# Layer 0 of a graph network: softmax weights and two operands of the counts held in a PSUM bank

## The chip, the cores and the metric

The kernel runs on one core of one Trainium2 chip, in one launch. The metric is device time in microseconds, the median of the timed runs. The engines are TensorE (PE in the profile, its weight loads PEld), VectorE (DVE), ScalarE (ACT), GpSimd (POOL) and SyncE (SP), which here only starts DMAs. Gathers by index are started by POOL.

## The reference, cut to what matters

Four graph layers run one after the other over 3125 nodes with 128 features and 100000 edges sorted by their destination. Each layer's result is added to its input and normalised. The change touches the first layer alone, a softmax-weighted sum over the edges that enter a node and the node itself:

```python
pre_edge = hP1[dst] + hP2[src] + zP3[edge_type]
logit_edge = _leaky(pre_edge) @ y_w                       # 8 heads
logits = jnp.concatenate([logit_self, logit_edge], axis=0)
mx = jax.ops.segment_max(logits, dst_a, num_segments=n)
ex = jnp.exp(logits - mx[dst_a])
denom = jax.ops.segment_sum(ex, dst_a, num_segments=n)
alpha = ex / denom[dst_a]
t_edge = hWh[src] + zWz[edge_type]
msg = (alpha[:, :, None] * t).reshape(-1, D)              # t in 8 heads of 16
agg = jax.ops.segment_sum(msg, dst_a, num_segments=n)
out = _leaky(agg + residual_weight * h)
```

The second layer averages node rows over the edges. The kernel computes it with a dense matrix of edge counts, which it builds while the first layer runs ("the counts").

## The kernel before, in words

The nodes are sorted by degree into 25 tiles of 128, one node a partition. Tile `t` has room for `CAP[t]` edges a node, 57 in the first and 21 in the last, 821 in all. A tile's edges are cut into chunks of at most 8 (`W`), 114 in all, and the chunks into runs of two or three, 49 in all.

For each edge of a chunk POOL starts one gather of 128 node rows into the tile `hs` (lines 102, 1207 and about). Each row holds 128 values for the attention, 128 values to be weighted and 8 logit parts. The relation rows `z` come in one of two ways: 77 chunks ("mult") make them by TensorE from one-hot matrices, the others gather them as `zs`, 205 gathers in all. TensorE adds up `pre`, ScalarE applies the leaky part, TensorE makes the 8 logits of each edge in PSUM (`lg`). VectorE adds the rest of a chunk's logits into the run's SBUF buffer `lgs` (L1360).

For a whole run `flow_run` then adds the mask (L1370), appends the node's old maximum as one more column (L1373), takes the new maximum (L1375), subtracts it (L1378) and lets ScalarE take the exponential in place (L1380). So `lgs` then holds `n` columns of 8 weights and, as column `n`, the factor `corr` for what was summed before. VectorE reads these: each chunk's values are multiplied by their weights (L970, in `spread`) and halved into one sum (L959, L963), which is added to the tile's sum (L1403); the tile's older sum is faded by `corr` (L833), the weights are summed into `sm` (L1391) and the denominator `l` is brought up to date (L1392, L1394).

Beside it `counts` builds the count matrix tile by tile. In `part_a` VectorE compares source numbers with all blocks (L615), runs a scan over the flags that counts them (L620), makes a base for each block from a matmul (L636, L639), adds it to the counts (L641), masks (L643) and reduces (L646). In `one_hots` (L568) VectorE compares digits with an index row `up` that lies in a PSUM tile, written by two TensorE transposes at the start (`count_up`) and from then on read by VectorE alone.

The order of the work on VectorE, ScalarE and TensorE in this layer is written out by hand. Each flow is a generator; `Plan.run` takes the one that is due first, lets it issue instructions until its next `yield`, and puts it back that many units later. `Room(n)` counts buffers: a flow that takes one while none is free is put back until another gives one. This decides the order of instructions when the kernel is built; on the chip each engine runs its queue in that order and waits for data. POOL and SP are not under this order.

```python
            A.activation(lgm, lgm, AF.Exp)
            yield 4
            corr = run.lg[:, n, :]
            for i, k in enumerate(run.chunks):
                plan.soon(1.5 * i, flow_spread(k))
```

Of the kernel before, what the change touches and what calls it, by code (L numbers as in the profile page):

```python
# [9 lines left out]
F32 = mybir.dt.float32  # L10
F16 = mybir.dt.float16
BF16 = mybir.dt.bfloat16
I32 = mybir.dt.int32
AF = mybir.ActivationFunctionType
OP = mybir.AluOpType
AX = mybir.AxisListType
# [3 lines left out]
P = 128  # L20
N = 3125
NT = 25
# [6 lines left out]
W = 8  # L29
# [5 lines left out]
H = 8  # L35
# [8 lines left out]
OFF = [sum(CAP[:t]) for t in range(NT + 1)]  # L44
NS = OFF[NT]
# [42 lines left out]
def tile_gnn(ctx, tc, a, out):  # L88
    nc = tc.nc
    V, A, G, T = nc.vector, nc.scalar, nc.gpsimd, nc.tensor  # L90
# [407 lines left out]
    with tc.tile_pool(name="srcp", bufs=1) as sp, tc.tile_pool(name="srcq", bufs=2, space=PSUM) as ps:  # L498
# [8 lines left out]
        for t in range(NT):  # L507
# [6 lines left out]
                                   op0=OP.add, op1=OP.mult)  # L514
            V.scalar_tensor_tensor(srcs[:, sl], pay_sb[:, sl, 0], float(-NP), live[:, :CAP[t]],
                                   op0=OP.add, op1=OP.mult)
# [10 lines left out]
        for o in range(0, NS, P):  # L527
            n = min(P, NS - o)
# [13 lines left out]
    blk0 = {}  # L542
# [8 lines left out]
    def count_up(pool, of):  # L551

        ri = pool.tile([P, 1], I32, name="c_ri")
        V.tensor_copy(ri, rowid)
        V.tensor_scalar(ri, ri, 1, None, op0=OP.arith_shift_right)
        rf = pool.tile([P, 1], F32, name="c_rf")
        V.tensor_copy(rf, ri)
        for k in range(2):
            row = pool.tile([P, P], BF16, name="c_row", bufs=2)
            V.tensor_scalar(row, onesb, rf, float(k * P // 2), op0=OP.mult, op1=OP.add)  # L560
            T.transpose(of[:, k * P:(k + 1) * P], row, identb)
        return of.rearrange("p (d s) -> p d s", s=2)
# [41 lines left out]
                if wait is not None:  # L604
                    self.soon(wait, steps)

    def counts(plan, begins, cp, ps, up, misc):


        def part_a(t):  # L610
            n, nb = CAP[t], NB[t]
            sl = slice(OFF[t], OFF[t + 1])
            oh = cp.tile([P, NT * max(CAP)], BF16, name="c_oh")[:, :NT * n]
            oh3 = oh.rearrange("p (j s) -> p j s", s=n)
            V.tensor_tensor(oh3, srchi[:, sl].unsqueeze(1).to_broadcast([P, NT, n]),  # L615
                            each_j[:, :, :n], op=OP.is_equal)
            yield 3
            inc = cp.tile([P, NT * max(CAP)], F32, name="c_inc")[:, :NT * n]
            inc3 = inc.rearrange("p (j s) -> p j s", s=n)
            V.tensor_tensor_scan(inc, oh, oh, 0.0, op0=OP.add, op1=OP.max)  # L620
            yield 4
            end = cp.tile([P, NT + 1], F32, name="c_end")
            G.memset(end[:, 0:1], 0.0)
            V.tensor_copy(end[:, 1:], inc3[:, :, n - 1])
            yield 3
            cnt = cp.tile([P, NT], BF16, name="c_cnt")
            V.tensor_sub(cnt, end[:, 1:], end[:, :NT])
            yield 3
            yield from misc.take()
            pre = ps.tile([P, 2, NT], F32, name="c_pre", tag="misc")  # L630
            T.matmul(pre[:, 0, :], upperb, cnt, start=True, stop=True)
            T.matmul(pre[:, 1, :], onesb, cnt, start=True, stop=True)
            yield 3
            V.scalar_tensor_tensor(crowd, pre[:, 1, :], float(-nb * P), crowd, op0=OP.add, op1=OP.max)
            bs = cp.tile([P, NT], F32, name="c_bs")
            V.tensor_sub(bs, pre[:, 0, :], end[:, :NT])  # L636
            misc.give()
            yield 3
            V.tensor_add(bs, bs, blk0[nb])  # L639
            yield 3  # L640
            V.tensor_add(inc3, inc3, bs.unsqueeze(2).to_broadcast([P, NT, n]))  # L641
            yield 3
            V.tensor_mul(inc3, inc3, oh3)  # L643
            yield 3
            pos = cp.tile([P, max(CAP)], F32, name="c_pos")
            V.tensor_reduce(pos[:, :n], inc.rearrange("p (j s) -> p s j", s=n), AX.X, OP.add)  # L646
            yield 4
            posi = cp.tile([P, max(CAP)], I32, name="c_posi")
            V.tensor_scalar(posi[:, :n], pos[:, :n], -1.0, None, op0=OP.add)
            yield 3  # L650
            dig = cp.tile([P, 2, max(CAP)], I32, name="c_dig")
            V.tensor_scalar(dig[:, 0, :n], posi[:, :n], 127, None, op0=OP.bitwise_and)
            V.tensor_scalar(dig[:, 1, :n], posi[:, :n], 7, None, op0=OP.arith_shift_right)
            yield 3
            digb = cp.tile([P, 2, max(CAP) + max(CAP) % 2], BF16, name="c_digb", bufs=2)
            V.tensor_copy(digb[:, :, :n], dig[:, :, :n])
            return digb
# [229 lines left out]
    with tc.tile_pool(name="l0", bufs=2) as wp, tc.tile_pool(name="l0s", bufs=1) as sp, \  # L887
# [78 lines left out]
        def spread(ac, hs, ex, n):  # L966

            val = hs[:, :n, D:2 * D]
            valh = val.rearrange("p s (h d) -> p s h d", h=H)
            V.tensor_tensor(valh, valh, ex.unsqueeze(3).to_broadcast([P, n, H, D // H]), op=OP.mult)  # L970
            yield 2.5
            yield from halves(hs[:, :, D:2 * D], n)
# [22 lines left out]
                except StopIteration as e:  # L995
                    return e.value

        up = count_up(cp, ps1.tile([P, 2 * P], BF16, name="c_up"))
        lg_at = ps1.tile([P, 2, 3 * W, H], F32, name="lg")
        misc = Room(1)  # L1000

# [148 lines left out]
        plan = Plan()  # L1150
        owns, selves, hws, hqs, azs, zbs, xs, shuts, x1s = map(Room, (1, 2, 3, 3, 4, 3, 5, 2, 3))
        hss, zss_, rbs, ohs_, zTs, zhs, zpss, pres, lows, tps, lgss = map(Room, (8, 3, 2, NK + 2, 2, 1, 1, 2, 2, 1, 3))
# [6 lines left out]
        class Run:  # L1159
            def __init__(self, tile_, k, run, behind_):  # L1160
                self.tile, self.k, self.behind, self.chunks = tile_, k, behind_, []
                self.s0, self.s1 = run[0][0], sum(run[-1][:2])
                self.n, self.lg, self.ex = self.s1 - self.s0, None, None
                self.summed = self.topped = self.totalled = False
                self.adds, self.faded = 0, False

        class Chunk:
            def __init__(self, run, s0, w, mult, g, start):
# [9 lines left out]
        for t in range(NT):  # L1178
            c = Tile(t)
# [3 lines left out]
            for run in runs(t):  # L1183
# [3 lines left out]
                for s0, w, mult in run:  # L1187
                    k = Chunk(R_, s0, w, mult, g, now)
# [5 lines left out]
        whole = now  # L1194
# [171 lines left out]
        def flow_run(run):  # L1366
            c, n, t = run.tile, run.n, run.tile.t
            o = OFF[t] + run.s0
            lg, lgm = run.lg[:, :n], run.lg[:, :n + 1]
            V.tensor_add(lg, lg, mask[:, o:o + n].unsqueeze(2).to_broadcast([P, n, H]))  # L1370
            while run.behind is not None and not run.behind.topped:
                yield 0.5
            V.tensor_copy(run.lg[:, n, :], m[:, t, :])  # L1373
            yield 2.5
            V.tensor_reduce(m[:, t, :], lgm.rearrange("p s h -> p h s"), AX.X, OP.max)  # L1375
            run.topped = True
            yield 2.5
            V.tensor_sub(lgm, lgm, m[:, t, :].unsqueeze(1).to_broadcast([P, n + 1, H]))  # L1378
            yield 1.5
            A.activation(lgm, lgm, AF.Exp)  # L1380
            yield 4
            corr = run.lg[:, n, :]
            for i, k in enumerate(run.chunks):
                plan.soon(1.5 * i, flow_spread(k))
            yield 1
            while run.behind is not None and (run.behind.adds or not run.behind.totalled):
                yield 0.5
            faded(c.ac, corr, H)
            run.faded = True
            sm = wp.tile([P, H], F32, name="sm")  # L1390
            V.tensor_reduce(sm, run.lg[:, :n].rearrange("p s h -> p h s"), AX.X, OP.add)  # L1391
            V.tensor_mul(l[:, t, :], l[:, t, :], corr)  # L1392
            yield 2.5
            V.tensor_add(l[:, t, :], l[:, t, :], sm)  # L1394
            run.totalled = True

        def flow_spread(k):
            run = k.run
            c, at = run.tile, k.s0 - run.s0
            yield from spread(c.ac, k.hs, run.lg[:, at:at + k.w], k.w)  # L1400
            while not run.faded:
                yield 0.5
            V.tensor_add(c.ac, c.ac, k.hs[:, 0, D:2 * D])  # L1403
            hss.give()
            run.adds -= 1
            if not run.adds:
                while not run.totalled:
                    yield 0.5
                lgss.give()
                if run is c.runs[-1]:  # L1410
                    while not c.self_done:
                        yield 1
                    plan.soon(2.5, close_b(c))
# [4 lines left out]
        for k in chunk_list:  # L1418
# [8 lines left out]
            for i in range(len(k.parts())):  # L1427
                plan.go(k.start + 1 + 4.5 * i, flow_pre(k, i))
            plan.go(k.start + 18, flow_lg(k))
        counts(plan, [0.95 * whole * OFF[t] / NS - 70 for t in range(NT)], cp, ps1, up, misc)  # L1430
        with tc.manual_schedule(engines=ORDERED | {mybir.EngineType.PE}):
            plan.run()
        assert hss.free == 8 and lgss.free == 3 and misc.free == 1 and shuts.free == 2 and x1s.free == 3
# [8 lines left out]
    with ExitStack() as ctx1, tc.tile_pool(name="l1", bufs=2) as wp, tc.tile_pool(name="l1s", bufs=1) as sp:  # L1442
# [14 lines left out]
        with tc.If(general > 0):  # L1457

            with tc.tile_pool(name="l1g", bufs=1) as gp, tc.tile_pool(name="l1gp", bufs=1, space=PSUM) as ps:
# [13 lines left out]
                for t in range(NT):  # L1473
# [6 lines left out]
                    with tc.For_i(0, trips, 1):  # L1480
# [10 lines left out]
                        at = gp.tile([P, W], F32, name="at")  # L1491
# [22 lines left out]
        ps1 = ctx1.enter_context(tc.tile_pool(name="l1p", bufs=1, space=PSUM))  # L1514
# [20 lines left out]
        with tc.tile_pool(name="l1pay", bufs=1) as pp:  # L1535
# [3 lines left out]
            for h in range(H2):  # L1539
                for k in range(3):  # L1540
                    V.scalar_tensor_tensor(bias[:, :, h], pays.bitcast(F32)[:, :, 3 + k],
                                           we[:, k * H2 + h:k * H2 + h + 1], mask if k == 0 else bias[:, :, h],
                                           op0=OP.mult, op1=OP.add)
# [574 lines left out]
```

## Time and profile before

| what | us |
|---|---|
| median of 3 timed runs | 5276.86 |
| lowest and highest of them | 5252.7 and 5283.75 |
| the profiled execution | 5264.1 |
| its span, first to last instruction | 5262.1 |
| busy in the span: PE, PEld | 2142.5, 1406.3 |
| busy in the span: DVE, ACT, POOL | 2924.2, 983.1, 2851.4 |

One execution was profiled. The page gives each engine's busy time, the span cut into 40 slices, and the costliest groups of instructions with their number, their mean duration and the idle time before them. A group is named by line, engine, operation and tiles, as out<-in; buffer numbers are left out. L102 is the helper that starts every gather, so gathers are told apart by their tiles. "remote" or "issue" as the cause of idle time means that the profile shows no instruction that ended the wait. Some matmul records are missing, so TensorE does somewhat more than its rows show.

### The profile page before, as it was taken

To read this page: it belongs to the slowest core of one execution; us is meant where nothing else is said; L and a number is where in the kernel's file an instruction comes from. 1 tells how busy PE (TensorE), PEld (TensorE's weight loads), DVE (VectorE), ACT (ScalarE), POOL (GpSimd) and SP (SyncE) were. 2 spreads that over 40 slices of the span, in tenths; PEclk is the share of its full clock that TensorE was granted. 3 is DMA by queue.
4 is the path that set the end of the run, shared out by engine and by line. 5 is a ranking of instruction groups with operands and counts; after the bars stand their busy time and mean duration, and the time that the engine had idled before them with its cause. 6 is when DMAs were issued, how large, how long until landed. Compare 5 with 4: busy or idle time off the path is not lost. (4 is left out here: it accounts for less than half of the span.)

```text
span 5262.1 us, 40042 instructions
## 1 busy us (share of the span) xinstructions
PE 2142.5 (41%) x12091; PEld 1406.3 (27%) x12091; DVE 2924.2 (56%) x6838; ACT 983.1 (19%) x2505; POOL 2851.4 (54%) x2922
## 2 busy tenths in 40 slices
PE   7166667677756677666480022222334000000000
PEld 5154545445544445444240011111111000000000
DVE  8355656566655566565523456656665355554555
ACT  1122233233323233322110011111111000000000
POOL 0544545546454344444217756666662777777774
PEclk9577788778777778777695555555557555555555
DMA  3422333333232222323343333333332333333331
GB/s 83 123 75 79 86 85 92 90 84 108 79 94 75 73 83 83 82 79 94 135 148 106 101 95 105 114 107 114 116 112 82 105 98 93 92 93 92 92 93 49
DMA packets 215514, 498.36 MB, mean 95 GB/s; under 512 B 62393, under 2 KB 112364, under 8 KB 210649
## 3 DMA queue, kind: packets, MB, share of 16 engines
q0 software_dynamic: 136448, 397.65, 26.7%
q1 hardware_dynamic: 78808, 97.76, 5.9%
q8 instruction: 102, 1.67, 0.1%
q14 instruction: 156, 1.28, 0.1%
HBM read 424.65 MB, written 70.63 MB: 94 GB/s over the span
## 5 line engine op out<-in xcount | busy, mean ns | idle before, releaser
L102 POOL DMA_INDIRECT hs<-h_tab,srcx x821 | 826.2, 1006 | 634.0 <-issue 395.7
L102 POOL DMA_INDIRECT kv<-ktv_tab,idx x821 | 852.5, 1038 | 283.5 <-issue 265.1
L102 POOL DMA_INDIRECT kv<-kv_tab,srcx x821 | 781.6, 952 | 368.3 <-issue 252.4
L1594 DVE TENSOR_TENSOR kv<-kv,qp 128x1024 f32<-128x1024 f32 (+4 forms) x228 | 253.1, 1110 | 694.7 <-DMA kv<-ktv_tab,idx 453.8
L102 POOL DMA_INDIRECT zs<-z_tab,rel x205 | 221.8, 1082 | 389.2 <-DVE zs L986 91.5
L1605 DVE TENSOR_REDUCE u<-kv 128x128 f32<-128x1024 f32 (+4 forms) x228 | 383.7, 1683 | 26.1 <-issue 19.7
L1248 PE MATMUL zps<-oh,zq 128*128 128x512 bf16 x1232 | 362.7, 440 | 57.0 <-issue 38.6
L568 DVE TENSOR_TENSOR c_ohs<-c_ends,c_up 128x1024 bf16<-128x1024 bf16 (+3 forms) x196 | 115.7, 591 | 315.8 <-remote 200.6
L949 PEld LDWEIGHTS pre<-ident,hs 128*128 128x128 f32 x1642 | 254.2, 219 | 130.0 <-issue 120.5
L1318 PE MATMUL t_ps<-zw,zT 128*128 128x136 f32 x1232 | 225.1, 318 | 155.8 <-DVE hs L1327 115.6
L949 PE MATMUL pre<-ident,hs 128*128 128x128 f32 x1642 | 256.6, 302 | 27.0 <-issue 24.3
L1597 DVE TENSOR_REDUCE lg<-kv 128x32 f32<-128x1024 f32 (+5 forms) x228 | 251.7, 1104 | 22.4 <-issue 22.2
L1601 DVE TENSOR_TENSOR kv<-kv,ex 128x1024 f32<-128x1024 f32 (+4 forms) x228 | 251.3, 1102 | 11.7 <-issue 11.7
L953 PE MATMUL lg<-yw,low 128*128 128x8 f32 x1642 | 238.8, 269 | 40.1 <-issue 24.2
L953 PEld LDWEIGHTS lg<-yw,low 128*128 128x128 f32 x1642 | 241.9, 222 | 48.6 <-issue 26.2
L678 ACT ACTIVATE c_oha<-c_oha,srclo 128x50 bf16<-128x50 bf16 (+2 forms) x821 | 211.7, 347 | 208.3 <-DVE c_oha L568 145.5
L1327 DVE TENSOR_TENSOR hs<-hs,t_ps 128x408 f32<-128x408 f32 (+1 forms) x231 | 121.2, 525 | 213.6 <-remote 58.4
L1318 PEld LDWEIGHTS t_ps<-zw,zT 128*128 128x128 f32 x1232 | 184.4, 214 | 183.1 <-issue 79.8
L837 PE MATMUL tp<-ident,an 128*128 128x128 f32 x25 | 11.3, 454 | 534.3 <-remote 465.1
L943 PE MATMUL pre<-identb,hq 128*128 128x512 bf16 (+3 forms) x645 | 205.8, 433 | 12.1 <-issue 12.1
L751 ACT ACTIVATE c_sb<-c_ps 128x512 bf16<-128x512 f32 (+1 forms) x175 | 96.3, 550 | 582.5 <-remote 259.1
L747 PE MATMUL c_ps<-c_ohs,c_ohd 128*128 128x128 bf16 x1300 | 127.0, 243 | 172.3 <-ACT c_sb L751 83.0
(418 smaller groups left out, 4785.2 us busy)
## 6 DMA issues: line engine op xcount, KB each, us to landing
rb<-rel_tab SPq DMA_DIRECT2D x77, 256.0 KB
c_tab<-c_sb SPq DMA_DIRECT2D x25, 768.0 KB
cs<-c_tab SPq DMA_DIRECT2D x6, 3200.0 KB
hs<-h_tab,srcx POOLq DMA_INDIRECT x821
kv<-kv_tab,srcx POOLq DMA_INDIRECT x821
kv<-ktv_tab,idx POOLq DMA_INDIRECT x821
h_tab<-h SPq DMA_DIRECT2D x25, 132.0 KB
zs<-z_tab,rel POOLq DMA_INDIRECT x205
```

What stands on the lines that cost most here:

```text
L102: return G.indirect_dma_start(out=dst, out_offset=None, in_=table, in_offset=indirect(idx), **kw)
L678: A.activation(oha[:, s // 2, 0, :, s % 2], oha[:, s // 2, 1, :, s % 2], AF.Copy, scale=srclo[:, o:o + 1])
L747: T.matmul(cps[:, j * P:(j + 1) * P], ohd[:, b // 2, :, b % 2], ohs[:, b // 2, :, b % 2], start=(i == 0), stop=(i == nb - 1))
L943: T.matmul(pre[:, :k], hq[:, i, :], identb.unsqueeze(1).to_broadcast([P, k, P]), start=(i == 0), stop=False)
L949: T.matmul(pre[:, s, :], hs[:, s0 + s, :D], ident, start=False, stop=(s == k - 1))
L953: T.matmul(lg_ps[:, s, :], low[:, s, :], yw8, start=True, stop=True)
L1248: T.matmul(zps, zq[:, i, 2 * R * k2:2 * R * (k2 + 1)], k.hot[i][:, cols], start=(i + k2 == 0), stop=(i == NK - 1 and k2 == 1))
L1318: T.matmul(t_ps[:, s, :], k.zT[:, (s0 + s) * P:(s0 + s + 1) * P], zw[:, D:], start=True, stop=True)
L1594: V.tensor_mul(k, k, qp.unsqueeze(1).to_broadcast([P, n, D]))
L1597: V.tensor_reduce(lg, kv[:, :n, :D].rearrange("p s (h d) -> p s h d", h=heads), AX.X, OP.add)
L1601: V.tensor_tensor(v, v, ex.unsqueeze(3).to_broadcast([P, n, heads, D // heads]), op=OP.mult)
L1605: V.tensor_reduce(u, kv[:, :n, D:].rearrange("p s d -> p d s"), AX.X, OP.add)
```

## The change

The index row's PSUM tile becomes a whole bank of 512 four-byte elements a partition. Its first 128 hold the index row as before. Three other things that VectorE reads come to lie in it:

- the weights of one run, `ex_at`. After the exponential, VectorE copies all `n + 1` columns of `lgs` there (up to 200 elements a partition). The multiplications, the fade, the sum and the product read the copy. Since there is room for one run, `exs = Room(1)` is taken before the copy and given back when the run's multiplications are issued and `l` is up to date. The `lgs` buffer is given back right after the copy, no longer after the run's last addition;
- the base `bs_at` of the counts, 25 elements, which one addition writes and the next reads;
- the scan's second operand. It was the flags themselves; it is now the first element of the index row, 0, repeated. The scan's second operation is a maximum, so the count, never below 0, is the same with either.

```diff
-            V.tensor_tensor_scan(inc, oh, oh, 0.0, op0=OP.add, op1=OP.max)
+            V.tensor_tensor_scan(inc, oh, up[:, 0, 0:1].to_broadcast([P, NT * n]), 0.0, op0=OP.add, op1=OP.max)
...
-            V.tensor_add(bs, bs, blk0[nb])
+            V.tensor_add(bs_at, bs, blk0[nb])
             yield 3
-            V.tensor_add(inc3, inc3, bs.unsqueeze(2).to_broadcast([P, NT, n]))
+            V.tensor_add(inc3, inc3, bs_at.unsqueeze(2).to_broadcast([P, NT, n]))
...
-        up = count_up(cp, ps1.tile([P, 2 * P], BF16, name="c_up"))
+        own_bank = ps1.tile([P, 4 * P], F32, name="c_up")
+        up = count_up(cp, own_bank.bitcast(BF16)[:, :2 * P])
+        ex_at = own_bank[:, P:P + (3 * W + 1) * H].rearrange("p (s h) -> p s h", h=H)
+        bs_at = own_bank[:, 3 * P:3 * P + NT]
+        exs = Room(1)
...
             A.activation(lgm, lgm, AF.Exp)
             yield 4
-            corr = run.lg[:, n, :]
+            yield from exs.take()
+            V.tensor_copy(ex_at[:, :n + 1], lgm)
+            lgss.give()
+            corr = ex_at[:, n, :]
...
-            V.tensor_reduce(sm, run.lg[:, :n].rearrange("p s h -> p h s"), AX.X, OP.add)
+            V.tensor_reduce(sm, ex_at[:, :n].rearrange("p s h -> p h s"), AX.X, OP.add)
...
             run.totalled = True
+            weights_read(run)
+
+        def weights_read(run):
+            if run.totalled and not run.mults:
+                exs.give()
...
-            yield from spread(c.ac, k.hs, run.lg[:, at:at + k.w], k.w)
+            steps = spread(c.ac, k.hs, ex_at[:, at:at + k.w], k.w)
+            yield next(steps)
+            run.mults -= 1
+            weights_read(run)
+            yield from steps
...
-                lgss.give()
```

More of the change, by code (lines that the diff above doesn't have):

```diff
@@ L605, in run, with counts @@
                     self.soon(wait, steps)
-    def counts(plan, begins, cp, ps, up, misc):
+    def counts(plan, begins, cp, ps, up, bs_at, misc):
         def part_a(t):
@@ L1164, in __init__ @@
                 self.summed = self.topped = self.totalled = False
-                self.adds, self.faded = 0, False
+                self.adds, self.mults, self.faded = 0, len(run), False
         class Chunk:
@@ L1429, in tile_gnn @@
             plan.go(k.start + 18, flow_lg(k))
-        counts(plan, [0.95 * whole * OFF[t] / NS - 70 for t in range(NT)], cp, ps1, up, misc)
+        counts(plan, [0.95 * whole * OFF[t] / NS - 70 for t in range(NT)], cp, ps1, up, bs_at, misc)
         with tc.manual_schedule(engines=ORDERED | {mybir.EngineType.PE}):
```

## The prediction, made before the changed kernel was run

> **What bounds the kernel now.** I read the busy time by stage first, since the change touches Layer 0 alone. The stages were cut at the first gather of node rows and at the last write of the layer's rows. Columns: length, then busy microseconds and instruction count of each engine, granted TensorE clock, DMA share, GB/s.
>
> ```profile
> core 0: us, PE busy (x) PEld busy (x) DVE busy (x) ACT busy (x) POOL busy (x), PEclk, DMA share, GB/s
> 0.00:200.00 200.00, 107.06 (x1002) 86.10 (x1002) 148.52 (x462) 20.91 (x70) 34.06 (x81) 0.85 0.34 99
> 200.00:2551.00 2351.00, 1569.28 (x9845) 1111.69 (x9845) 1358.94 (x3880) 693.65 (x1861) 1082.10 (x1100) 0.77 0.31 84
> ...
> 2900.00:3950.00 1050.00, 263.77 (x453) 115.20 (x453) 624.93 (x1188) 129.15 (x262) 699.16 (x733) 0.55 0.36 108
> 3950.00:5262.10 1312.10, 53.20 (x125) 23.92 (x125) 666.81 (x1008) 112.69 (x220) 885.08 (x853) 0.52 0.31 89
> ```
>
> Layer 0 is the 2351 us row. TensorE is busy 67% of it, VectorE 58%, POOL 46%. The last two rows are Layers 2 and 3, where POOL leads with 67%. So POOL, the engine this change can relieve, is third in the stage where it is to be relieved. The chain that ended last says nothing here: it lies in Layer 3.
>
> Second, what TensorE waited for inside that stage (who, by whom, total, times, longest):
>
> ```profile
> PE t_ps L1318 <- DVE hs L1327: 115.6, 54, 12.3
> PE c_ps L747 <- ACT c_sb L751: 83.0, 21, 15.9
> ...
> PE sl_ps L1068 <- DVE rest L1139: 28.8, 2, 22.2
> ...
> PE pre L949 <- DMA hs<-h_tab,srcx: 1.7, 1, 1.7
> ```
>
> TensorE idles 2351 - 1569 = 782 us. Adding up all lines of this view that name VectorE gives about 260 us, a third. Gathered rows ended 1.7 us of it, and 5.3 us before the weight loads of the same line. Counted over the 734 first uses of gathered rows between 260 and 2310 us, the rows had landed a median of 12 us before TensorE took them. Late gathers are not what Layer 0 waits for.
>
> Third, the gathers by duration (min/median/max in ns), and one place in the order of time where they are slowed:
>
> ```profile
> L102 POOL DMA_INDIRECT hs<-h_tab,srcx x821: 940/946/2825, 199.3 to 2456.2; - x165
> L102 POOL DMA_INDIRECT kv<-kv_tab,srcx x821: 940/946/1543, 2767.5 to 3941.6; - x165
> ```
>
> ```profile
> 1004.38 1.21 DVE L970 TENSOR_TENSOR hs<-hs,lgs 128x1024 f32<-128x1024 f32 x1
> ...
> 1005.14 1.61 POOL L102 DMA_INDIRECT hs<-h_tab,srcx  x1 [0.30 <-issue]
> 1005.52 0.41 DVE L959 TENSOR_TENSOR zh<-zh 128x256 f32<-128x256 f32 x1
> ...
> 1007.05 0.95 POOL L102 DMA_INDIRECT hs<-h_tab,srcx  x1 [0.30 <-issue]
> ```
>
> A gather needs 0.946 us. The one that ran beside two VectorE instructions with both inputs in SBUF took 1.61 us; the next, alone, 0.95. The page has the mean of the 821 `hs` gathers at 1006 ns and of the 205 `zs` gathers at 1082. The 821 of Layer 2, where the weights already come from PSUM, have 952. So the effect the change aims at exists. VectorE itself is not held up: its group `hs<-hs,lgs` shows no idle time before it.
>
> **The change, part by part.** Fourth, VectorE groups with their shapes (busy us, mean ns, then idle before):
>
> ```profile
> L970 DVE TENSOR_TENSOR hs<-hs,lgs 128x1024 f32<-128x1024 f32 x92 | 111.9, 1216 | 0.0
> L1601 DVE TENSOR_TENSOR kv<-kv,ex 128x1024 f32<-128x1024 f32 x184 | 222.4, 1209 | 6.6 <-issue 6.6
> L1360 DVE TENSOR_TENSOR lgs<-lg,hs 128x64 f32<-128x64 f32 x92 | 19.8, 215 | 19.1 <-remote 13.3 <-PE c_perm L688 3.2 <-PE lg L953 1.5
> L989 DVE TENSOR_TENSOR az<-az,zs 128x64 f32<-128x64 f32 x37 | 7.9, 214 | 0.0
> L1378 DVE TENSOR_TENSOR lgs<-lgs,m 128x200 f32<-128x200 f32 x14 | 5.0, 359 | 0.0
> L1864 DVE COPY xqb<-qkv 128x128 f32<-128x128 f32 x25 | 6.1, 243 | 13.6 <-ACT qkv L1852 13.4
> ```
>
> *Added: one copy a run.* There are 49 runs (L1373 stands 49 times). The copy has the shape of the subtraction on L1378, whose 49 took a median of 292 ns: 49 x 0.292 = 14.3 us is the upper end. No copy into PSUM is in the trace. The lower end is L1373's 8-element copy, 169 ns: 8.3 us. Between 169 ns at 8 elements and 243 at 128 the mean copy of 142 elements costs 0.25 us; I take 0.27, nearer to the row of its own shape, so 13 us. A neighbour that reads what was just written starts 0.03 us after its end in the records, an unrelated one 0.08 us before it: 0.11 x 49 = 5.7 us at most, and 3 taken, as other work often stands between. Together 16 us of VectorE, between 8 and 20. Everything behind the copy in VectorE's fixed order waits too, above all the `hs` addition L1327 that gives TensorE its `t_ps` buffer back. The wait for the exponential only moves from the first multiplication to the copy in front of it.
>
> *Moved to PSUM: 114 multiplications, 49 fades, 49 sums, 49 products.* L970 against L1601 is the same shape with the small operand in SBUF and in PSUM: 1216 and 1209 ns. At 64 elements L989 and L1360 say 214 and 215. So 0, between -1 and +1 us. [...]
>
> *The counts' base:* 25 additions of 25 elements that write PSUM, 25 additions (25.2 us) that read it. 0 by the same pairs of rows.
>
> *The scan:* 25 instructions, 46.5 us, 1247 to 3128 ns from 525 to 1425 elements, so 2.09 ns an element, where the additions on L641 take 1.06 (1062 to 1646 ns from 875 to 1425). If the second stream is what doubles it, a one-element operand saves up to 21 us; if PSUM is dear there, a few us are added. The scan at L286, with other types, has the same slope (425 ns for 128), so I take 0 and keep -21 to +3.
>
> *The gathers.* All that could be lost to VectorE in the stage is (1006 - 946) x 821 + (1082 - 946) x 205 = 77 us. Laying each gather over the VectorE rows it overlapped, the excess falls to L970 (about 15 us), the scan (14) and L641 (7): 36 us that POOL would save. The halving additions, the `zs` additions and others keep both inputs in SBUF and the rest of the excess. [...] On TensorE's path lie 1.7 + 5.3 us of waits for landings; I take 3 us of gain, between 0 and 36.
>
> *The room for one run's weights and the earlier return of the logits' buffer.* Neither alters the written order: in the trace each run's last multiplication and its update of `l` end before the next run's first multiplication starts, and by the written due times a logits buffer is free whenever a run takes one. 0. If the room bound, the next run's copy, and in the written order all that follows it, would stand behind the earlier run's update of `l`, 3.4 us after its first multiplication in the first run.
>
> **Sum.** VectorE's 16 us reach the end in part: a third by its share of TensorE's idle time, all of it where the chain runs through VectorE. I take half, +8, between +3 and +20. Less 3 for gathers: +5 us. The profiled execution took 5264.1 us (span 5262.1 and 2.0 around it), 12.8 below the median of the three timed runs, 5276.86, which themselves spread over 31 us. 5264.1 + 5 = 5269, or 5282 from the median; I forecast the middle, 5276.
>
> **Rivals.**
> *Faster:* POOL's saving counts in full and the scan loses its second stream: 36 + 21 - 8 = 49 us, 5227. For it: the lengthened gathers at 1004 us, and Layer 2's 952 ns. Against it: 12 us of slack and 7 us of waits for landings. It needs more than 53 us to leave the 1% band, so also gathers that now queue behind one another; 0.12.
> *Slower:* POOL's order. DVE, ACT and PE are in hand-written order, POOL and SP are not; 49 new copies may shift where a POOL instruction that waits for VectorE stands among the gathers. The clearing of `x` (L909) already waits 84.3 us for VectorE in 7 places, 27.0 at the longest, with gathers queued behind. With 12 us of slack one more such wait costs TensorE up to 15 us; from four on it passes 53 us: 5276 + 60 = 5336. Nothing in the diff touches those instructions, so 0.14.
> *The change doesn't do what it says:* `hs` gathers stay at 1006 ns, as other both-in-SBUF work takes the place. Then +8 instead of +5, 5279; this is inside the forecast's band, 0.15 of its 0.74.
>
> **How the numbers follow.** 1% (53 us) is about what a measurement of this kernel can tell from no change. Forecast and third rival 0.74, faster 0.12, slower 0.14. The range runs from 5276 - 40 (the gathers' 36 us on the path and copies nearly hidden) to 5276 + 34 (all 20 us of copies on the path, and one displaced POOL wait of 14): 5236 to 5310.
>
> **What would show it.** Right: 49 copies of 0.25 to 0.30 us into `c_up`; L970's successor within 20 ns of 1216; the `hs` mean near 970 ns; POOL some 36 us less busy in Layer 0; that stage within 25 us of 2351; Layers 1 to 3 alike. Wrong: a stage shorter by over 50 us with TensorE's waits for VectorE much smaller, which would mean that the gathers held the stage in a way the waits don't show; or longer POOL waits at L909 and TensorE waiting for landings.

## The result, and the profile after

The change took 5308.12 us, the median of six runs (5307.16 to 5326.16), against 5269.37 us for the kernel before in the same comparison. The ratio is 1.0088 with a 95% interval of 1.0065 to 1.0112: slower by 39 us between the medians, and by 46 us (34 to 59) by the ratio and its interval, where +5 was worked out. The time lies in the predicted range and the ratio within 1%, but the rise is real and the sum does not explain it. The profiled execution of the changed kernel is the longest of the six, 5326.16 us with a span of 5324.2; the one of before took 5264.1. So the two profiles lie 62 us apart, further than the medians.

The busy time by stage, with the same columns as before the change:

```profile
core 0: us, PE busy (x) PEld busy (x) DVE busy (x) ACT busy (x) POOL busy (x), PEclk, DMA share, GB/s
0.00:200.00 200.00, 107.18 (x1002) 86.09 (x1002) 148.57 (x460) 21.13 (x70) 34.31 (x81) 0.85 0.34 99
200.00:2614.00 2414.00, 1587.55 (x9845) 1128.78 (x9845) 1368.43 (x3925) 693.97 (x1861) 1051.64 (x1099) 0.76 0.30 82
...
4010.00:5324.20 1314.20, 51.84 (x125) 23.17 (x125) 667.66 (x1008) 112.70 (x220) 888.03 (x854) 0.52 0.31 89
```

Layer 0 is 2414 us, 63 more than in the profile before; the last two layers are as they were. In it VectorE is 9.5 us busier, POOL 30.5 us less busy. Of VectorE's time the 49 copies are 14.8 us. The 49 sums of the weights, which now read the copy, give 4.7 us back (18.9 before, 14.2 after). Both edits show up, and neither is near 63 us.

The gathers (min/median/max in ns), two VectorE groups with their shapes (busy us, mean ns, then idle before), and the sums before and after (min/median/max in ns):

```profile
L102 POOL DMA_INDIRECT hs<-h_tab,srcx x821: 943/949/2132, 199.1 to 2529.6; - x165
...
L102 POOL DMA_INDIRECT zs<-z_tab,rel x205: 943/949/1850, 201.7 to 2516.5; - x103
```

```profile
L970 DVE TENSOR_TENSOR hs<-hs,c_up 128x1024 f32<-128x1024 f32 x92 | 111.8, 1215 | 0.6
...
L833 DVE TENSOR_TENSOR az<-az,c_up 128x128 f32<-128x128 f32 x49 | 13.7, 280 | 0.0
```

```profile
L1391 DVE TENSOR_REDUCE sm<-lgs x49: 270/376/500, 332.4 to 2527.5; 128x8 f32<-128x192 f32 x14, 128x8 f32<-128x128 f32 x13, 128x8 f32<-128x72 f32 x4, 128x8 f32<-128x120 f32 x3
...
L1398 DVE TENSOR_REDUCE sm<-c_up x49: 226/284/357, 331.9 to 2592.8; 128x8 f32<-128x192 f32 x14, 128x8 f32<-128x128 f32 x13, 128x8 f32<-128x72 f32 x4, 128x8 f32<-128x120 f32 x3
```

The longest `hs` gather fell from 2825 to 2132 ns, the mean of the 821 from 1006 to 990 and that of the 205 `zs` gathers from 1082 to 1007. The multiplications take 1215 ns as against 1216. The 49 copies (L1387) take 0.30 us each.

What grew stands in the list of waits (who, by whom, total us, times, longest), first two lines of before and then those of the change:

```profile
ACT c_sb L751 <- remote: 259.1, 29, 19.3
...
DVE c_ohs L568 <- remote: 200.6, 23, 18.0
```

```profile
ACT c_sb L751 <- remote: 377.8, 36, 20.6
DVE c_ohs L568 <- remote: 255.0, 23, 17.5
...
PE c_ps L747 <- ACT c_sb L751: 105.4, 22, 16.0
...
PE t_ps L1322 <- DVE hs L1331: 92.4, 44, 15.1
```

The last two were 83.0 and 115.6 before: TensorE's wait for VectorE, through which the copies were expected to act, fell. The two largest waits for which the profile names nobody grew by 119 and 54 us. Two others of the kind fell, ScalarE's `low` (L1300, now L1304) from 154.0 to 126.0 and VectorE's `c_ohb` (L568) from 150.3 to 114.1, so the list alone does not say what the layer lost. In order of time, one of those that grew:

```profile
2330.04 0.91 PE L1322 MATMUL t_ps<-zw,zT 128*128 128x136 f32 x6
...
2331.13 0.95 POOL L102 DMA_INDIRECT hs<-h_tab,srcx  x1 [0.30 <-issue]
2332.39 0.94 POOL L102 DMA_INDIRECT hs<-h_tab,srcx  x1 [0.31 <-issue]
...
2341.14 0.95 POOL L102 DMA_INDIRECT hs<-h_tab,srcx  x1 [0.30 <-issue]
2342.09 0.22 POOL L909 MEMSET x<- 128x128 f32 x1
2342.24 0.12 POOL L623 MEMSET c_end<- 128x1 f32 x1
2342.59 1.01 POOL L102 DMA_INDIRECT x<-in_x,node_d  x1 [0.23 <-POOL c_end L623]
2346.32 0.60 ACT L751 ACTIVATE c_sb<-c_ps 128x512 bf16<-128x512 f32 x1 [19.08 <-remote]
2346.32 0.69 DVE L568 TENSOR_TENSOR c_ohs<-c_ends,c_up 128x1024 bf16<-128x1024 bf16 x1 [17.29 <-remote]
...
2346.97 0.80 PE L747 MATMUL c_ps<-c_ohs,c_ohd 128*128 128x128 bf16 x6 [16.02 <-ACT c_sb L751]
```

From 2331 to 2346 us nothing runs on TensorE, VectorE or ScalarE, while POOL starts one gather after another until 2343.6 us. ScalarE's copy L751 waits for matmuls that had ended by 2331 us; it starts 2.7 us after POOL's last gather has ended. I call this a standstill: time in Layer 0 (from the first `hs` gather to the last write of the layer's rows) in which none of PE, PEld, DVE and ACT has a record. Added up over the layer, from the records:

| kernel | Layer 0 | standstill | the rest |
|---|---|---|---|
| before | 2347 | 433 | 1914 |
| the change | 2412 | 492 | 1920 |

The part in which some engine works is 6 us longer, as the prediction's sum has it. The other 59 us are standstill. The prediction's reading had no such item: it counted idle time engine by engine, and none of its sums uses a wait for "remote".

### The profile page after: what moved, and what is told of

Same layout as the page of the kernel before. It is cut to its first block, busy times and chain, and to the rows that moved or that the text cites. A ratio compares the mean times of both kernels' runs of the same rounds, so it can differ in the third digit from the quotient of the medians.

```text
span 5324.2 us, 40114 instructions
## 1 busy us (share of the span) xinstructions
PE 2155.9 (40%) x12091; PEld 1420.4 (27%) x12091; DVE 2931.2 (55%) x6887; ACT 983.7 (18%) x2505; POOL 2825.3 (53%) x2922
## 5 line engine op out<-in xcount | busy, mean ns | idle before, releaser
L102 POOL DMA_INDIRECT hs<-h_tab,srcx x821 | 812.6, 990 | 676.2 <-issue 439.9
L102 POOL DMA_INDIRECT zs<-z_tab,rel x205 | 206.5, 1007 | 421.8 <-DVE zs L986 101.2
L949 PEld LDWEIGHTS pre<-ident,hs 128*128 128x128 f32 x1642 | 260.7, 223 | 150.4 <-issue 138.8
L568 DVE TENSOR_TENSOR c_ohs<-c_ends,c_up 128x1024 bf16<-128x1024 bf16 (+3 forms) x196 | 115.9, 593 | 329.5 <-remote 255.0
L949 PE MATMUL pre<-ident,hs 128*128 128x128 f32 x1642 | 265.3, 307 | 40.2 <-issue 38.9
L751 ACT ACTIVATE c_sb<-c_ps 128x512 bf16<-128x512 f32 (+1 forms) x175 | 96.3, 551 | 697.8 <-remote 377.8
```

What stands on the lines that cost most here:

```text
L102: return G.indirect_dma_start(out=dst, out_offset=None, in_=table, in_offset=indirect(idx), **kw)
L949: T.matmul(pre[:, s, :], hs[:, s0 + s, :D], ident, start=False, stop=(s == k - 1))
```

## The experiments

The runs fell into two kinds of job. In the first kind the kernel before takes 5269 to 5312 us, in the second 4333 to 4339, with the same program. VectorE and ScalarE are equally busy in both (1359 and 694 us of Layer 0 in the first profile, 1357 and 690 in `e5`); TensorE (1569 and 1390 us) and the `hs` gathers (1006 and 1116 ns) are not. The expectations speak of two kinds of chip; since a job of either kind named chip number 8, the runs do not tell whether the kind belongs to the chip, its machine or the hour. A ratio is always against before in the same job.

### Which part costs it (first kind, before 5298.62 us)

`e1`: the weights' copy and its readers, with scan and base as before:

```diff
-            V.tensor_add(bs_at, bs, blk0[nb])
+            V.tensor_add(bs, bs, blk0[nb])
...
-            V.tensor_tensor_scan(inc, oh, up[:, 0, 0:1].to_broadcast([P, NT * n]), 0.0, op0=OP.add, op1=OP.max)
+            V.tensor_tensor_scan(inc, oh, oh, 0.0, op0=OP.add, op1=OP.max)
```

> The weights' copy and their readers as in the change; scan and counts' base as before. This kernel has the 49 copies, and its SyncE order is that of before (the whole change has one pair swapped there: the last piece of a count row stands behind the load of a later tile's sums). Theory C, the copies cost the whole rise because every wait between VectorE, TensorE and ScalarE behind them is stretched: +35 to +45 us against before, Layer 0 as long as with the change. Theory S, the swapped pair on SyncE costs most of it: +5 to +15 us here. Theory P, reading the weights from PSUM is dear: as C here, but not where the copies go unread.

5327.48 us, ratio 1.0057 (1.0040 to 1.0074): +29 us.

`e2`: the kernel before with only the copy added (`V.tensor_copy(ex_at[:, :n + 1], lgm)` behind the exponential).

> The kernel before with the 49 copies into the PSUM bank added; nothing reads them, all readers use lgs, and the lgs buffer is given back as before. SyncE order as before. Theory C: +30 to +45 us, as much as the copies with their readers. Theory P (PSUM readers are dear): +5 to +15 us. By the prediction's term for the copies: +3 to +20 us. Theory S: +5 to +15 us. The hs gathers stay near 1006 ns here, since the multiplications keep both inputs in SBUF.

5309.26 us, 1.0020 (1.0004 to 1.0036): +11 us. `hs` gathers at 1009 ns, as before.

`e3`: scan and base from PSUM, no copies; `e4`: the scan's operand alone, the diff's scan line and nothing else.

> Scan operand and counts' base from the PSUM bank, weights as before: no copy. It has the swapped pair on SyncE. Theory S: +25 to +40 us. Theory C: 0 to +5 us. By the prediction's terms for both: -21 to +3 us, taken as 0.

> Only the scan's second operand is the one PSUM element; order of every engine, SyncE too, as before. All theories 0 within 5 us; if the scan's operand matters, its 25 instructions (46.5 us) change by up to 20 us and the time with them, and the gathers beside the scan come to 0.95 us each.

`e3` 5340.31 us, 1.0076 (1.0047 to 1.0105); `e4` 5333.85 us, 1.0066 (1.0047 to 1.0084): +35 us. This answered none of the theories. In `e4` no instruction is added, the order on every engine is that of before, and the 25 scans take 46.4 us in all as against 46.5. Beside longer standstills, the difference that its records show is in the gathers beside the scan: `hs` 989 ns on average. The base and the swapped pair on SyncE, which `e3` has and `e4` has not, make 6 us between the medians, less than the intervals can tell. Theories C, P and S fell. Nor do the parts add up: `e1` and `e3` together make 71 us, the whole change made 39 in its job.

### Is it the change at all? (second kind, before 4332.97 us)

`e5` is the kernel before against itself. `e6` is `e4` with the element in an SBUF tile of zeros (`none[:, 0:1]` for `up[:, 0, 0:1]`), `e7` the base alone, `e8` the whole change.

> The kernel before, unchanged, as a control, with a profile from the same chip as the experiments. The four kernels run so far, even the one that only changed the scan's operand, lag behind the first profile of before in the same staircase (about +10 us by 515 us, +30 by 985 us). Theory K (the changes cause the lag): ratio 1.000, and this profile runs as the first one, within 5 us at 985 us. Theory N (the lag belongs to the execution, not to the change): this profile shows part of the staircase too, 10 to 30 us at 985 us. Theory L (each load of a program has its own time, and differences of 0.5% mean nothing): the ratio leaves 1.000 by over 0.003.

> As the run that changed the scan's operand alone, but the one element lies in SBUF (a tile of zeros) instead of PSUM. Same order on every engine. If the PSUM operand cost the +35 us: within 5 us of before. If what costs is that the scan no longer streams two SBUF operands and the gathers beside it get quicker: +30 to +40 us, hs gathers near 990 ns. If it was no effect of the operand at all: anything.

> Only the counts' base goes to the PSUM bank; scan and weights as before. It has the swapped pair on SyncE. If the pair is what cost in the run with scan and base: +35 to +45 us. If the scan is: 0 to +10 us.

> The whole change once more on the chip of the experiments. The first comparison gave 1.0088 (1.0065 to 1.0112). If the parts add, scan +35, base and swap +6, copies and weights +30: +70 us, 1.013. If they share one cause that can cost only once: +35 to +50 us.

0.9992 (0.9983 to 1.0000), 0.9993 (0.9982 to 1.0004), 0.9979 (0.9970 to 0.9987) and 0.9987 (0.9978 to 0.9995). In this kind of job the change costs nothing that the control doesn't show as well. Layer 0 of `e5`, and under it that of `e8`:

```profile
199.00:1872.00 1673.00, 1389.67 (x9842) 1024.11 (x9842) 1357.13 (x3873) 689.67 (x1859) 1193.55 (x1099) 0.89 0.43 118
```

```profile
199.00:1862.00 1663.00, 1412.80 (x9843) 1039.56 (x9843) 1364.25 (x3919) 690.02 (x1860) 1091.82 (x1098) 0.88 0.44 119
```

VectorE is as busy as in the first profile (1357 and 1359 us), yet the layer is 674 us shorter. The standstill is 51 us here and 35 with the change, against 433 in the first profile, which makes 382 of the 674 us. In the rest TensorE is busy for 1390 us instead of 1569 with the same instructions, at a granted clock of 0.89 instead of 0.77. The list of waits of `e5` names a releaser nearly everywhere: ScalarE's `c_sb` waits 320.0 us for `c_ps` and none for "remote". The relief of the gathers is far larger than in the first profile: more of them overlap VectorE in the shorter layer (125 of the 1026 overlap nothing of it, 497 in the first profile), POOL drops by 102 us (`hs` 1116 to 1025 ns, `zs` 1173 to 1046), and still the time gains nothing that could be told from the control, with TensorE 83 and 85% busy and VectorE 81 and 82%. The swapped pair on SyncE, which `e7` has, costs nothing here (0.9979). With the one SBUF element (`e6`) `hs` stays at 1114 ns as against 1116, so that operand brings no relief.

### The controls once more (first kind, before 5298.05 us)

`e9` is before against itself, `e10`, `e11` and `e12` are `e4`, `e2` and `e1` again.

> The kernel before against itself once more. Two kinds of chip have shown up: one on which before takes 5270 to 5300 us, and one on which it takes 4333 us; the control has run only on the second (0.9992). If this job falls on the first kind: theory K (the parts cause the +0.6 to +0.9% seen there) wants 1.000 within 0.002; theory L (every load of a program has its own time there) wants a ratio off 1 by over 0.003 either way. On the second kind: 1.000 within 0.001.

> Scan's second operand alone from PSUM, a second time. On the first kind of chip: 1.0066 again by theory K, anything between 0.997 and 1.008 by theory L. On the second kind: same order, same durations of its scans, gathers beside them shorter; 0 to -10 us, and hs gathers some 30 us of POOL shorter in all (there the mean was 1116 ns before and 1025 with the whole change).

> The 49 copies into the PSUM bank that nobody reads. On the first kind: 1.002 again by theory K. On the second kind VectorE is busy for over 80% of Layer 0, so most of the copies' 13 to 18 us should show: +8 to +18 us (1.002 to 1.004); by the prediction's term +3 to +20; 0 if TensorE alone sets the time there. Gathers as before (near 1116 ns).

> Copies and their readers, scan and base as before. On the first kind: 1.0057 again by theory K. On the second kind: as the unread copies, less what the quicker gathers give back: the difference between the two is the whole worth of the relief. By the prediction -3 us (0 to -36); hs gathers near 1050 ns.

1.0005 (0.9986 to 1.0024), 1.0033 (1.0013 to 1.0053), 1.0021 (1.0002 to 1.0040) and 1.0038 (1.0021 to 1.0056). The control lies on 1, the parts do not. But the scan alone came out at 15 us where it had been 35, so between two jobs of this kind a ratio moves by 0.3%, more than its interval says. Layer 0 taken apart for all profiles of this kind:

| kernel | Layer 0 | standstill | the rest | `hs`, `zs` mean ns |
|---|---|---|---|---|
| before, `e9` before | 2347, 2384 | 433, 464 | 1914, 1920 | 1006, 1082; 1013, 1100 |
| copies unread: `e2`, `e11` | 2388, 2392 | 462, 451 | 1926, 1941 | 1009, 1070; 1015, 1077 |
| weights: `e1`, `e12` | 2413, 2393 | 495, 478 | 1918, 1915 | 999, 1047; 1000, 1050 |
| scan: `e4`, `e10` | 2423, 2393 | 525, 480 | 1898, 1913 | 989, 1082; 1005, 1096 |
| scan and base: `e3` | 2421 | 512 | 1909 | 994, 1076 |
| the change | 2412 | 492 | 1920 | 990, 1007 |

Against the control of their own job the unread copies (`e11`) lengthen the rest by 21 us and not the standstill. `e2` has no profile of before from its job; its standstill lies 2 us below one profile of before and 29 above the other. Every kernel that moves an operand to PSUM has a longer standstill: by 14 us (`e12`) and 16 us (`e10`) against the control of their own job, and by 28 us (the change) to 61 us (`e4`) in the others, counted from that same control. Before itself shows 433 and 464 us in its two executions, so a single difference of this size proves little; that all six profiles lie above both is what counts. The standstill does not grow in step with the relief, though: the change has the quickest gathers and less standstill than `e3` and `e4`, and the gathers of `e10` are in sum no quicker than in the first profile of before, where the standstill is 47 us less.

### Where the standstills are

A train is a run of at least 8 POOL instructions with less than 0.7 us between them. Standstill in Layer 0 by place, each time as us of standstill in us of that place:

| kernel | first 5 us of a train | the rest of it | 4 us behind it | elsewhere |
|---|---|---|---|---|
| before | 1 in 219 | 362 in 1018 | 67 in 176 | 5 in 933 |
| `e9` before | 2 in 229 | 384 in 1012 | 76 in 184 | 4 in 958 |
| the change | 1 in 229 | 390 in 995 | 95 in 184 | 4 in 1003 |
| `e5` before, second kind | 5 in 83 | 43 in 1401 | 1 in 76 | 3 in 112 |

In the first kind of job a good third of the time in and just behind a train is lost, after its first 5 us (429 of 1194 us in before), and next to nothing elsewhere (5 of 933 us). In the second kind more of the layer lies in trains (1484 us as against 1237) and next to nothing is lost (44 of 1477 us after the first 5 us). So I tried whether the trains cause it, by thinning them: POOL clears the slot before it starts the gather into it. This leaves the order on all other engines as it was.

```diff
+                    G.memset(k.hs[:, s, :], 0.0)
                     gather(k.hs[:, s, :], h_tab, srcx[:, k.o + s:k.o + s + 1])
```

> The kernel before, with a memset of the slot (264 elements) on POOL ahead of each of the 821 hs gathers: the gathers of a train follow one another some 0.4 us later each, POOL is busy some 300 us longer, the order of all other engines is the same. Theory G (dense trains of gathers cause the standstills on the first kind of chip): standstills in Layer 0 fall from some 450 us by 100 us or more, and the time by 50 us or more. If the standstills have another cause: as many as before, the time 0 to +60 us. On the second kind of chip (before 4333 us) there is little to save: 0 to +40 us.

> Two such memsets ahead of each hs gather, some 0.8 us each time. Theory G: on the first kind of chip a still smaller standstill than with one, though the gathers come so late that TensorE may wait for them: the time between -150 and +50 us. Another cause: +50 to +200 us. On the second kind: +100 us or more, since POOL is then busy all through the layer.

> The whole change with one memset ahead of each hs gather. Theory G: the change's extra standstill goes with the trains, so this kernel stands within 15 us of before with one memset. If the change costs by itself: 30 to 50 us above it.

These three fell on the second kind (before 4335.68 us): 1.0225 (1.0207 to 1.0243), 1.0659 (1.0641 to 1.0676) and 1.0104 (1.0084 to 1.0124). There is little standstill to win there, and with the clears it grows: from 51 us in `e5` to 91 in `e13` and 211 in `e14`, the one with two clears. The layer now waits more for gathers: in the waits of `e13`, VectorE's L981 waits 114 us for their landings, where in `e5` it waited 55.

```profile
DVE hs L981 <- DMA zs<-z_tab,rel: 59.8, 5, 32.0
...
DVE hs L981 <- DMA hs<-h_tab,srcx: 54.6, 15, 8.6
```

Where POOL is this busy (81% of Layer 0 in `e13`), the relief pays: the change with one clear takes 4376.18 us, before with one clear 4431.31, 55 us less, with 99 us less of POOL. The same kernel of before with one clear, once more:

> The kernel before with one memset of the slot on POOL ahead of each hs gather, once more, for the first kind of chip (before 5270 to 5300 us). Theory G: standstills in Layer 0 below 350 us and the time 50 us or more below before. Another cause: standstills 430 us or more, the time at or above before. On the second kind of chip: +96 us as before.

This job was of the first kind: 4805.42 us against 5311.98, ratio 0.903 (0.8996 to 0.9065), 507 us less. Its Layer 0, and a line of its waits:

```profile
203.00:2085.00 1882.00, 1481.64 (x9738) 1082.28 (x9843) 1375.70 (x3870) 694.39 (x1859) 1411.30 (x1918) 0.84 0.39 105
```

```profile
ACT c_sb L751 <- remote: 97.9, 21, 11.0
```

POOL does 821 more instructions and is 329 us busier than before, and the layer is 465 us shorter than in the first profile. The standstill is 97 us, the rest 1785. Against the profile of `e9` that is 367 us less standstill and 134 us less of the rest, at a granted clock of 0.84 instead of 0.76. POOL is now busy for 75% of the layer; 1483 us of it lie in trains behind their first 5 us, with 93 us of standstill: 0.06 per microsecond instead of 0.36. From one gather's start to the next's (counting steps below 4 us) the mean is 1.34 us in before, 1.31 with the change, and 1.61 with the clears. The clears do two things at once, they space the gathers and put an instruction of another kind between them; no run tells these apart.

`e17` is `e15` again, `e18` the change with a clear ahead of every second gather (`if s % 2:` before the memset).

> The whole change with one memset ahead of each hs gather. First kind of chip (before near 5300 us): before with the same clears took 0.903 of before. If the change loses only through standstills: 0.89 to 0.905, and Layer 0 with about 100 us of standstill. If it costs by itself there: 0.911 or more. Second kind: 1.010 as before.

> The whole change with a memset ahead of every second hs gather. First kind of chip: if the standstill grows steadily with the density of the trains, halfway, 0.94 to 0.96; if there is a density below which it ends, near 0.90. Second kind: POOL 150 us busier instead of 250, below the +40 us of the full thinning: 0 to +20 us.

Both met the second kind (before 4339.46 us): 1.0103 (1.0081 to 1.0126) and 0.9994 (0.9983 to 1.0005). Half the clears cost nothing there that could be told from before. What the change does with thinned trains in the first kind of job was not measured, so no version is shown to beat both kernels in both kinds.

## Why the prediction was right or wrong

**The copies.** Taken at 0.27 us each and 13 us in all, they measure 0.30 and 14.8. Taken as +8 of the end, bounds +3 to +20, unread copies cost 11 and 14 us (`e2`, `e11`). The size held, a little small. The way did not show: TensorE's wait for the `hs` addition, through which they were to act, is 101.2 us in `e11` and 110.2 in the control of its job. One product of this part is off without effect: 0.11 x 49 is 5.4 us, not 5.7.

**What moved to PSUM.** 0 was right for the multiplications and the fades: 1215 against 1216 ns at L970, 280 against 283 at L833. It was wrong for the 49 sums, which have no row of their own in the prediction: with the weights in PSUM their median is 284 ns instead of 376, 4.7 us less in all, outside the -1 to +1 that was kept. That it is the reading and not the copy shows in `e2`, where the copy goes unread and the sums stay at 376, and in `e1`, where they read it and take 283. The 25 scans take 46.4 us against 46.5, the 25 additions that read the base 25.0 against 25.2, and the 25 that write it 4.7 against 4.4.

**The relief of the gathers.** As a description it held: `hs` to 990 ns (near 970 was said), POOL 30.5 us less in the layer (36 was said), waits of TensorE for landings small before and after (1.7 and 1.0 us at the matmuls of L949). The 5.3 us that were added to the 1.7 contain them; the weight loads alone waited 3.5 us. It is also no matter of POOL's order, which is unchanged: its waits at L909 are 82.8 us against 84.3, so the slower rival, which put 60 us there, did not occur. The rival that the change doesn't do what it says fell with the 990 ns.

**The step that failed** is the price of this relief: "On TensorE's path lie 1.7 + 5.3 us of waits for landings; I take 3 us of gain, between 0 and 36." The bounds let it gain or do nothing. In the kind of job where the comparison was made, the parts that bring it lose: the scan's operand alone, which adds no instruction and keeps every order, costs 35 and 15 us, and the copies with their readers cost 18 and 7 us more than the copies alone (the 7 us are within the intervals). Behind it lies a term that the sum does not have. Of the 782 us that TensorE idled, the prediction accounted for some 260 by VectorE and 7 by landings; its sum has nothing for the remainder, without a reason. The 259 us of "remote" at L751 and 201 at L568 were the largest waits of ScalarE and VectorE in the layer, and they enter nowhere. An overlay of all engines would have shown 433 us in which none of the three worked, nearly all of it in and behind POOL's trains; with the change it is 492.

**What is shown and what is not.** Shown: in the profiles the rise is standstill and not work (59 of 65 us against the first profile of before, 28 of 28 against the control's); standstills lie in and just behind trains of gathers (430 of 433 us in the first profile); in the first kind of job a clear between the gathers does away with most of them (97 us left of 464), and with 507 us. In the second kind of job, with little standstill (51 us), the change costs nothing (0.9987). Not shown: why the change lengthens the standstills, and that it does so by denser trains. An estimate from these rows comes near for the change: one clear a gather took 464 - 97 = 367 us of standstill for 329 us of POOL, 1.1 us each; the change takes 30.5 us off POOL and should by that add 34 us, where its profile has 28 to 59 and the medians say 39. It fails for the scan alone: there the gathers are 14 us shorter in all, which makes 16 us, and the standstill of `e4` is 61 to 92 us longer. The run that would have tested it, the change with thinned trains in the first kind of job, did not come about. Nor is it known how a train holds the others up. Every run here was recorded with its span and clock, so the runs cannot tell whether the recording has a part in the standstills.

**The faster rival** did not occur: 49 us was its estimate where POOL's saving counts in full. The change does bring 55 us once clears make POOL busier (`e13` to `e15`), but that the two figures are near is chance: the 49 held 21 us for a scan that did not get faster, and POOL saved 99 us there, not 36.

**The band.** "About what a measurement of this kernel can tell from no change" was 1%; six runs a side told 0.9% from nothing, while the ratio of the scan alone moved by 0.3% from one job to another. The whole change was measured in one job of the first kind only.

## What to carry to other kernels

Before pricing an edit, lay the engines over one another and ask when none of them works; a wait with no named releaser is time to be explained, and what runs on the remaining engine during it is the first suspect. Relieving an engine that is off the path can cost: in one kind of job here every kernel with an operand moved to PSUM took 15 to 42 us more, and a clear ahead of each gather, which spaces the gathers, took 507 us off. That the two are the same effect is not shown. A control of the kernel against itself, and the same kernel in several jobs, belong to any result under one per cent.

## What the runs showed of the hardware

The same program took 4333 us in some jobs and 5300 in others, at mean granted clocks of 0.70 and 0.66, with Layer 0 at 1673 us (`e5`) and 2384 us (`e9`). In the 4 us behind the 31 standstills of over 3 us in the first profile of before, the granted clock was 0.52 on average, against 0.77 over the layer. In the profiles of the first kind of job many semaphore updates are missing in the records: 4086 of 5173 for VectorE's semaphore in before, against 5169 of 5173 in `e5`. `e16` has as few (3979 of 5174) and only 97 us of standstill, so the missing records do not measure the standstill by themselves.

The 414 `hs` gathers that overlap nothing of VectorE in the first profile of before took 940 to 955 ns. From one gather's start to the next's, 761 steps of 1025 lay between 1.225 and 1.275 us there. Behind the first 5 us of a train the other engines stood still for 0.36 us per microsecond in that profile, and for 0.03 in `e5`, with a median `hs` gather of 946 and 947 ns. Adding 821 POOL memsets, 251 and 252 us, made the kernel 507 us faster in one job (`e16`) and 96 us slower in another (`e13`). The sums of 24 weights for each of 8 heads (`sm`, 14 of the 49) took 351 ns each from PSUM (the profile of the change) and 492 from SBUF (that of before).
